# The product of exchanged keys in a windowed attention: made by GpSimd, ahead of the sums that it makes already

## The chip, the cores and the metric

The kernel runs on one core of a Trainium2 chip. A core has five engines that run independently and wait for each other through semaphores: TensorE (matrix products, from SBUF into PSUM), VectorE (called DVE in the profile), ScalarE (ACT), GpSimd (POOL) and SyncE (SP, which here only issues DMAs). The metric is the device time of one execution in microseconds, and the median of several runs. Before the change it is 934.08 us, the median of 3 runs (932.01 to 934.68).

## The reference, cut to what matters

The program is two layers on 4096 tokens (16 sequences of 256) of width 128, all in float32. A layer adds an attention and a mixture of experts to its input. The change lies in the attention of layer 0, for which this is what is computed:

```python
qk, v = split(layernorm(xn) @ w_qkv.T)           # 8 heads of 64; queries and keys are the same projection
bq, bk = buckets(qk) * 64 ** -0.5, look_around(buckets(qk))   # windows of 128
bq = bq * cos(qf) * qs + rotate_half(bq) * sin(qf) * qs
bk = bk * cos(freqs) / scale + rotate_half(bk) * sin(freqs) / scale
sim = where(mask, NEG, bq @ bk.T)
out = softmax(sim) @ bv
out = out.reshape(b, n, 512) @ w_out.T
```

`rotate_half` exchanges the two halves of a head's 64 channels and changes one sign. So a rotated query or key is the sum of two products: the projection times a table of cosines, and the exchanged projection times a table of sines (the sign and the scale are in the tables). The expert part of layer 0 needs a router on the same normalised tokens; layer 1 has a gated attention and 32 experts of its own.

## The kernel before

**Layout.** In attention the channels lie on the 128 partitions (two heads of 64) and the tokens along the free axis. The tokens are worked in 8 groups of 512 (two sequences). For each group there are 4 pairs of heads, so there are 32 *rotations*, n = 0 to 31, each with a tile of 128 x 512 for queries and one for keys. A rotation serves two *steps*, one for each sequence of the group: scores, softmax and product with the values for two heads of one sequence. The loop `for s in range(-3, NS + 1)` (line 547) runs over the 64 steps with three steps of lead.

**A rotation** is in `rotated(n)`, in four parts that are called in different steps:

- TensorE makes the projection `pq` in PSUM (line 381) in an odd step, s = 2n - 7.
- `copied` (lines 391 to 394), in the next step: ACT copies `pq` to the tile `here` in SBUF, and SyncE issues four DMAs that write its blocks of 32 partitions, exchanged, to the tile `there`.
- `near` (line 398), in the same step: DVE makes `q` and `k`, the products of `pq` with the cosine tables. One operand is in PSUM.
- `far` (line 402), in step 2n - 5: DVE makes `sq` and `sk`, the products of `there` with the sine tables. Both operands are in SBUF. The table covers one sequence and is repeated for the second by a broadcast.
- `sums` (line 406), in the same step: `q` plus `sq`, then `k` plus `sk`. For 0 < n < `FREE` = 23 GpSimd makes them, otherwise DVE.

The tiles for `sq`, `sk`, `here` and `there` have two buffers each, those for `q` and `k` three. Scores that use rotation n are first made in step 2n - 3.

**A step** s, in the order in which the kernel is written: TensorE transposes the attention weights of step s (line 460) and ACT copies them out of PSUM (line 467); ACT takes the exponentials of step s + 2 (line 437); DVE does `near` of a rotation where one is due; DVE divides the weights of step s + 1 by their sums, a reciprocal (line 443) and three multiplications of 128 x 256 in SBUF (line 446; ACT does the fourth, line 451); pieces of the layer norm and of the router for a later group; `far`; the scores of step s + 3 on TensorE (line 421), and on DVE four instructions that mask them and take the row maxima out of PSUM (line 427); `sums`; then the product with the values for step s - 1 (line 477), and the projections of later rotations and groups.

**The pieces.** For each group the layer norm and the router are cut into pieces that are put into fixed steps (dictionary `pieces`, line 517), five steps apart from one group to the next. Two of them use GpSimd: `moments` (line 152) and `again` (line 169) raise a 128 x 4 tile to the power -0.5 there, after a short computation on DVE.

**Order.** All this stands under a manual schedule for TensorE, DVE, ACT and GpSimd: each engine executes its instructions in the order in which the program issues them, and waits are added where the data ask for them. From step 41 on GpSimd also issues indirect DMAs that scatter tokens to the experts (line 317); each of these waits for an instruction of ACT in the same step. `FREE` = 23 ends GpSimd's sums before that: rotation 22 is summed in step 39. SyncE issues, beside the exchanges, loads and the zeroing of the scatter's target (line 610).

Of the kernel before, what the change touches and what calls it, by code (L numbers as in the profile page):

```python
# [15 lines left out]
ALU = mybir.AluOpType  # L16
# [31 lines left out]
def two_layers(ctx: ExitStack, tc: tile.TileContext, a: dict, out: bass.AP):  # L48
    nc = tc.nc
# [16 lines left out]
    def mm_tile(name):  # L66
        tags, n = turn
        turn[1] += 1
        return bank(tags[n % len(tags)], name)
# [4 lines left out]
    def load(name, shape, src=None, eng=None, pool=const):  # L74
        t = pool.tile(shape, F32, tag=name, name=name)
        (eng or nc.scalar).dma_start(out=t, in_=a[name] if src is None else src)
        return t
# [17 lines left out]
    sink = load("sink", [P, N], pool=w_a, eng=sp)  # L95
# [236 lines left out]
    with first as pa:  # L332
# [35 lines left out]
        def over(t):  # L368
            return t.unsqueeze(1).to_broadcast([P, 2, N])
# [4 lines left out]
        FREE = 23  # L374

        def rotated(n):

            g, hp = divmod(n, 4)
            h = slice(hp * P, (hp + 1) * P)
            pq = mm_tile(f"pq_{g}_{hp}")  # L380
            nc.tensor.matmul(pq, wqk[:, h], xhTs0[g], start=True, stop=True)
            heads[n] = got = [
                wk.tile([P, 2, N], F32, tag=f"rot{what}", name=f"{what}_{g}_{hp}", bufs=3) for what in "qk"
            ]
            parts = [wk.tile([P, 2, N], F32, tag=f"rots{what}", name=f"s{what}_{g}_{hp}") for what in "qk"]
            here = wk.tile([P, 2, N], F32, tag="here", name=f"here_{g}_{hp}")
            there = wk.tile([P, 2, N], F32, tag="there", name=f"there_{g}_{hp}")

            def copied():

                nc.scalar.copy(here.rearrange("p b n -> p (b n)"), pq)
                for q in range(0, P, 32):
                    to = q ^ 32
                    nc.sync.dma_start(out=there[to : to + 32], in_=here[q : q + 32])

            def near():
                for t, m in zip(got, (cosq, cosk)):
                    nc.vector.tensor_tensor(t, pq.rearrange("p (b n) -> p b n", n=N), over(m), ALU.mult)

            def far():  # L400
                for t, m in zip(parts, (sinq, sink)):
                    nc.vector.tensor_tensor(t, there, over(m), ALU.mult)

            def sums():
                for r, part in zip(got, parts):
                    (nc.gpsimd if 0 < n < FREE else nc.vector).tensor_tensor(r, r, part, ALU.add)  # L406

            later.append(copied)
            turning.append([near, far, sums])


# [89 lines left out]
        with tc.manual_schedule(engines={order.PE, order.DVE, order.Activation, order.Pool}):  # L501
# [45 lines left out]
            for s in range(-3, NS + 1):  # L547
# [60 lines left out]
                if s >= 2 and s % 2 == 0 and s - 2 < NT0:  # L608
                    n = min(2, NT0 - (s - 2))
# [511 lines left out]
```

## Time and profile before

| what | us |
|---|---|
| median of 3 runs | 934.08 (932.01 to 934.68) |
| the profiled execution's own time | 934.61 |
| its span, first to last instruction | 932.8 |
| TensorE busy | 890.2 (95%) |
| DVE busy | 695.9 (75%) |
| ACT busy | 495.4 (53%) |
| GpSimd busy | 280.5 (30%) |
| rotations 1 to 22, `sq` of the first to `sk` of the last | 24.4 to 234.1 |
| scatters of layer 0, first to last start | 242.8 to 339.5 |

The profile is of one execution. Busy time is when an engine's datapath works; register, branch and semaphore instructions and the issue of DMAs do not count. L402 is line 402 of the kernel before. A row for a group of instructions gives the line, the engine, the operation, what it writes and reads (out<-in, buffer numbers left out), the shapes, the count, the busy time and the mean duration of one in nanoseconds, the idle time of the engine just before them and what ended that. A row of the timeline gives start, duration, engine, line, operation and the count of instructions merged into it. Starts are in us from the first instruction. A matmul's end is modelled, and a busy TensorE is not one at its peak; spans on GpSimd are rough.

### The profile page before, as it was taken

To read this page: it belongs to the slowest core of one execution; us is meant where nothing else is said; L and a number is where in the kernel's file an instruction comes from. 1 tells how busy PE (TensorE), PEld (TensorE's weight loads), DVE (VectorE), ACT (ScalarE), POOL (GpSimd) and SP (SyncE) were. 2 spreads that over 40 slices of the span, in tenths; PEclk is the share of its full clock that TensorE was granted. 3 is DMA by queue.
4 is the path that set the end of the run, shared out by engine and by line. 5 is a ranking of instruction groups with operands and counts; after the bars stand their busy time and mean duration, and the time that the engine had idled before them with its cause. 6 is when DMAs were issued, how large, how long until landed. Compare 5 with 4: busy or idle time off the path is not lost.

```text
span 932.8 us, 13465 instructions
## 1 busy us (share of the span) xinstructions
PE 890.2 (95%) x3762; PEld 506.0 (54%) x3762; DVE 695.9 (75%) x2283; ACT 495.4 (53%) x1228; POOL 280.5 (30%) x251
## 2 busy tenths in 40 slices
PE   2999999999999999989999999999999999999997
PEld 1456666565555547888545454454544545445453
DVE  4999999899999933333688686885868858678563
ACT  1688998798898873334443423434234342434411
POOL 2343333322467640001524231242312423121200
PEclk8899999999999999999999999999999999999999
DMA  7171010110122228984172434315343144331430
GB/s 199 27 235 43 24 35 24 25 34 24 44 77 66 69 73 265 260 231 133 29 159 60 112 91 94 91 48 113 90 90 93 49 107 97 81 87 42 104 91 11
DMA packets 70441, 84.54 MB, mean 91 GB/s; under 512 B 14944, under 2 KB 45408, under 8 KB 70240
## 3 DMA queue, kind: packets, MB, share of 16 engines
q1 hardware_dynamic: 65840, 74.76, 31.1%
q0 software_dynamic: 4096, 8.40, 3.0%
q8 instruction: 31, 0.51, 0.2%
q10 hardware_dynamic: 432, 0.53, 0.2%
q14 instruction: 42, 0.34, 0.1%
HBM read 58.22 MB, written 17.04 MB: 81 GB/s over the span
## 4 chain that ended last, share of the span: by engine, by line
PE 61%; DVE 22%; ACT 6%; DMA 4%; issue 3%; SPq 2%; POOL 1%; DVEq 0%; ACTq 0%
PE z L1001 9%; PE g L964 8%; PE u L966 8%; DVE p L427 4%; PE s L421 4%; PE o L477 3%; DVE p L446 3%; PE o L939 3%; PE yr L691 3%; PE h L680 3%; PE t L460 2%; ACT r1s L905 2%; PE y L490 2%; DMA xt<-x_rows 2%; PE z L1019 2%
## 5 line engine op out<-in xcount | busy, mean ns | idle before, releaser
L968 ACT ACTIVATE h<-g 128x512 f32<-128x512 f32 x128 | 75.1, 592 | 204.7 <-PE g L964 201.9
L970 DVE TENSOR_TENSOR h<-h,u 128x512 f32<-128x512 f32 x128 | 86.5, 681 | 61.4 <-PE u L966 45.9
L966 PE MATMUL u<-xn1Ts,eu 128*128 128x512 f32 x256 | 130.8, 593 | 1.2 <-DVE h L970 1.2
L964 PE MATMUL g<-xn1Ts,eg 128*128 128x512 f32 x256 | 130.8, 593 | 0.0
L437 ACT ACTIVATE p<-p,nm 128x256 f32<-128x256 f32 x256 | 127.5, 514 | 0.2 <-DVE nm L427 0.2
L1001 PE MATMUL z<-h,ed 128*128 128x512 f32 x224 | 115.3, 598 | 1.6 <-DVE h L973 0.9
L762 POOL DMA_INDIRECT yg<-y_rows,slot_at x64 | 65.8, 1028 | 117.6 <-PE hs L627 99.0
L973 DVE TENSOR_TENSOR h<-h,bc 128x512 f32<-128x512 f32 x128 | 97.7, 770 | 2.3
L427 DVE CUSTOM_DVE_ANT_0 p<-s,mask 128x256 f32<-128x256 f32 x256 | 92.8, 418 | 2.5 <-PE s L421 2.5
L421 PE MATMUL s<-k,q 64*128 64x256 f32 x512 | 84.3, 411 | 8.7 <-DVE k L406 6.0
L966 PEld LDWEIGHTS u<-xn1Ts,eu 128*128 128x128 f32 x256 | 48.5, 190 | 61.1 <-issue 52.3
L460 PEld LDWEIGHTS t<-ident,p 128*128 128x128 f32 x512 | 59.4, 141 | 35.0 <-issue 8.3
L317 POOL DMA_INDIRECT x_rows<-xn_all,slot_at x64 | 67.1, 1049 | 36.9 <-ACT pT L467 16.0
L467 ACT COPY pT<-t 128x512 f32<-128x512 f32 x128 | 69.2, 597 | 10.4 <-PE t L460 10.4
L1001 PEld LDWEIGHTS z<-h,ed 128*128 128x128 f32 x224 | 41.5, 190 | 55.9 <-issue 39.1
L964 PEld LDWEIGHTS g<-xn1Ts,eg 128*128 128x128 f32 x256 | 46.9, 191 | 45.2 <-issue 39.4
L910 POOL TENSOR_TENSOR r1s<-r1s,sinr 128x512 f32<-128x512 f32 x16 | 21.0, 1312 | 166.4 <-ACT r1s L905 166.3
L477 PE MATMUL o<-pT,v 128*64 128x256 f32 x512 | 70.3, 396 | 0.3 <-ACT oT L482 0.2
L460 PE MATMUL t<-ident,p 128*128 128x128 f32 x512 | 67.3, 274 | 1.4 <-ACT p L451 1.4
L421 PEld LDWEIGHTS s<-k,q 64*128 64x128 f32 x512 | 51.0, 188 | 26.6 <-DVE nm L427 9.0
L446 DVE TENSOR_SCALAR p<-p,sm 128x256 f32<-128x256 f32 x208 | 62.1, 357 | 2.3
L683 ACT ACTIVATE h0s<-h,we 128x256 f32<-128x256 f32 x78 | 32.7, 470 | 53.6 <-issue 43.8
(264 smaller groups left out, 1510.2 us busy)
## 6 DMA issues: line engine op xcount, KB each, us to landing
bc<-rows_r SPq DMA_DIRECT2D x128, 256.0 KB, 4.4
there<-here SPq DMA_DIRECT2D x128, 64.0 KB, 2.0
we<-in_ex_dram SPq DMA_DIRECT2D x39, 129.0 KB, 3.9
xt<-x_rows SPq DMA_DIRECT2D x39, 128.0 KB, 3.9
y_rows<-yt SPq DMA_DIRECT2D x39, 128.0 KB, 3.7
x_rows<-zero SPq DMA_DIRECT2D x19, 256.0 KB, 3.3
x<-in_x_dram SPq DMA_DIRECT2D x8, 256.0 KB, 5.8
out_dram<-out SPq DMA_DIRECT2D x8, 256.0 KB, 2.3
```

Source lines behind the costliest of these rows:

```text
L421: nc.tensor.matmul(sp[h][:, i, :], q[rows, b, i * P : (i + 1) * P], k[rows, b, :], start=True, stop=True)
L427: nc.vector.tensor_tensor_reduce(out=pr[:, h, i, :], in0=sp[h][:, i, :], in1=mask[:, i, :], scale=-1.0, scalar=-NEG, op0=ALU.add, op1=ALU. ...
L437: paces[1] = nc.scalar.activation(row, row, AF.Exp, bias=nm[:, n : n + 1], scale=-1.0, accum_out=sm[:, n : n + 1])
L446: nc.vector.tensor_scalar(row, row, sm[:, n : n + 1], None, ALU.mult)
L460: nc.tensor.transpose(tp[:, at : at + P], pr[:, h, i, j * P : (j + 1) * P], ident)
L477: nc.tensor.matmul(op[h * DH : (h + 1) * DH, :], vs[g][:, 2 * b + j, (2 * hp + h) * DH : (2 * hp + h + 1) * DH], pT[:, h, j, :], start=(j ...
L964: nc.tensor.matmul(gp, wg, xn1Ts[g], start=True, stop=True)
L966: nc.tensor.matmul(up, wu, xn1Ts[g], start=True, stop=True)
L968: nc.scalar.activation(h, gp, AF.Silu)
L970: nc.vector.tensor_tensor(h, h, up, ALU.mult)
L973: nc.vector.tensor_tensor(h, h, spread_w[g][n // 2][:, n % 2, :], ALU.mult)
L1001: nc.tensor.matmul(zp, w, r, start=(n == 1), stop=False)
```

## The change

In `far` the second product, that of the exchanged keys with their sine table, is issued on GpSimd for rotations 1 to 22, and on DVE as before for rotations 0 and 23 to 31. The product of the exchanged queries stays on DVE. The call stays where it was, so on GpSimd the product stands after whatever the pieces of that step have issued there, and ahead of the two sums of the same rotation.

```diff
             def far():
                 for t, m in zip(parts, (sinq, sink)):
-                    nc.vector.tensor_tensor(t, there, over(m), ALU.mult)
+                    eng = nc.gpsimd if m is sink and 0 < n < FREE else nc.vector
+                    eng.tensor_tensor(t, there, over(m), ALU.mult)
```

Everything else is unchanged: tables, buffers, the places of the calls, and the DMAs.

## The prediction

> **What bounds the kernel now.** The change touches rotations 1 to 22 of the attention stage, so I first read busy times by stretch, cut where VectorE (DVE) begins to have idle time. Columns: stretch and length, then each engine's busy time and count, TensorE clock, DMA share, GB/s.
> ```profile
> 28.00:68.00 40.00, 37.07 (x212) 21.95 (x210) 38.95 (x165) 34.71 (x107) 14.71 (x13) 0.99 0.46 145
> 68.00:98.00 30.00, 30.00 (x187) 18.84 (x188) 28.85 (x120) 27.02 (x85) 11.42 (x10) 1.00 0.16 43
> 98.00:127.00 29.00, 29.00 (x178) 18.04 (x177) 28.25 (x117) 26.17 (x82) 10.68 (x9) 1.00 0.11 27
> 127.00:168.00 41.00, 39.21 (x246) 24.24 (x242) 40.09 (x169) 37.41 (x117) 16.10 (x13) 1.00 0.12 30
> 168.00:200.00 32.00, 32.00 (x192) 19.05 (x192) 27.38 (x108) 27.27 (x86) 8.49 (x6) 0.95 0.11 28
> 200.00:236.00 36.00, 35.32 (x203) 21.16 (x202) 34.14 (x138) 31.29 (x96) 10.86 (x8) 1.00 0.10 25
> ```
> From 28 to 168 us DVE is busy 136.1 of 140 us. In the timeline its only gaps over 0.08 us are 1.06 at 28 and 0.18, 0.34 and 0.12 later; the rest are 0.02 to 0.05 between dependent instructions. So DVE sets the pace there, although TensorE looks full too and the chain of waits runs through TensorE from 67 to 127. From 168 to 236 DVE is idle 6.5 us and TensorE leads. DVE time added before 168 therefore lengthens the run nearly one for one; time removed helps only until TensorE leads.
>
> Next the groups that move (count, busy us, mean ns, idle before), on GpSimd (POOL) and on DVE:
> ```profile
> L406 POOL TENSOR_TENSOR q<-q,sq 128x512 f32<-128x512 f32 x22 | 33.1, 1506 | 85.3 <-DVE sq L402 70.7 <-PE t L460 8.5 <-PE s L421 6.0
> L406 POOL TENSOR_TENSOR k<-k,sk 128x512 f32<-128x512 f32 x22 | 28.0, 1271 | 0.0
> ```
> ```profile
> L402 DVE TENSOR_TENSOR sk<-there,sink 128x512 f32<-128x512 f32 x32 | 21.9, 683 | 0.0
> ```
> GpSimd has room: the stretches above hold 72 us of its work in 208. But why is the first sum 0.24 us dearer than the second? It starts while DVE still runs sk. That sent me to places where both engines use SBUF together (start, duration), in layer 1:
> ```profile
> 494.20 1.25 POOL L783 TENSOR_TENSOR x<-x,xn 128x512 f32<-128x512 f32 x1
> ```
> ```profile
> 494.26 1.87 DVE L173 TENSOR_SCALAR xh<-xn,brs 128x128 f32<-128x128 f32 x4 [1.12 <-POOL brs L169]
> ```
> ```profile
> 530.46 1.27 POOL L910 TENSOR_TENSOR r1s<-r1s,sinr 128x512 f32<-128x512 f32 x1
> 531.80 1.59 POOL L912 TENSOR_TENSOR r<-r,r1s 128x512 f32<-128x512 f32 x1
> ```
> ```profile
> 531.10 2.84 DVE L973 TENSOR_TENSOR h<-h,bc 128x512 f32<-128x512 f32 x2
> ```
> Four L173 take 0.86 alone (149.12) and 1.87 here: blocked until 0.18 before the GpSimd sum ends. Two L973 take 1.29 when free (the same shape in L970) and 2.84 here: the first waits 0.48 for L910; then L912, which has been waiting, gets in between the two, and the second waits 1.07. So SBUF-to-SBUF work of either kind on DVE stops while a large GpSimd sum runs. Reductions from PSUM do not: L427 keeps 0.42 under every sum. The 123 divisions L446 before 235 us take 345 to 356 ns each, because no sum of theirs collides: the two sums now fit between sk and the next division, where DVE works from PSUM (L427, L398).
>
> **The change part by part.**
> *Removed from DVE*: one sk per rotation. Starts lie 0.60 apart, so 0.60 each.
> *Added to GpSimd*: one product, 1.27 us by the row r1s<-r1s,sinr (1272 median, same shape, same broadcast factor). Its queue is pow, product, q sum, k sum. The product waits for the exchanged keys, whose DMAs land some 4.4 us after the ACT copy, mostly before DVE reaches sq. So it runs before sq, and what it collides with depends on where the pow of the layer norm (L152, L169) stands.
>
> *Group A, rotations 2, 3, 7, 8, 12, 13: the pow comes one step earlier.* Rotation 2:
> ```profile
> 32.07 1.02 POOL L152 TENSOR_TENSOR brs_a<-bve_a,mhalf 128x4 f32<-128x4 f32 x1 [4.05 <-DVE bve_a L150]
> ```
> ```profile
> 33.52 0.88 DVE L446 TENSOR_SCALAR p<-p,sm 128x256 f32<-128x256 f32 x3
> 34.31 1.11 DVE L158 TENSOR_SCALAR xn_all<-x,bmv_a,brs_a 128x128 f32<-128x128 f32 x4
> 35.34 0.69 DVE L402 TENSOR_TENSOR sq<-there,sinq 128x512 f32<-128x512 f32 x1
> ```
> The keys have landed at 31.9, so the product runs from 33.07 to 34.34. L446 wants to start at 33.52 and starts at 34.16: 0.64 lost, 0.60 saved. For rotation 3 the loss is 0.68. Net +0.06 each, +0.4 for six.
>
> *Group B, rotations 4, 5, 9, 10, 14, 15: the pow is in the same step.* Rotation 4:
> ```profile
> 54.70 0.69 DVE L402 TENSOR_TENSOR sq<-there,sinq 128x512 f32<-128x512 f32 x1
> ...
> 58.69 0.88 DVE L446 TENSOR_SCALAR p<-p,sm 128x256 f32<-128x256 f32 x3
> ```
> ```profile
> 54.75 1.52 POOL L152 TENSOR_TENSOR brs_a<-bve_a,mhalf 128x4 f32<-128x4 f32 x1 [5.47 <-DVE bve_a L150]
> 56.25 1.27 POOL L406 TENSOR_TENSOR q<-q,sq 128x512 f32<-128x512 f32 x1
> 57.48 1.27 POOL L406 TENSOR_TENSOR k<-k,sk 128x512 f32<-128x512 f32 x1
> ```
> The product takes the place of the q sum at 56.25 and pushes the sums to 57.48 and 58.71. L446 comes at 58.09 without sk: it waits for the q sum until 58.57 (0.48), and the k sum gets in among the three divisions, 1.07 as at 531.80. Loss between 0.48 (the divisions stay together) and 1.55; I take 1.55, since the row shows the GpSimd operation entering. Net +0.95. Rotation 15 loses its share after 168, where DVE has idle time, and only its 0.60 counts: 5 x 0.95 - 0.6 = +4.15.
>
> *Group C, rotations 6 and 11: no pow near.* The product starts at the landing (70.7, 120.2) and holds the small two-operand L226 up (71.25 to 71.84); loss 0 to 1, net taken as 0. *Rotations 16 to 22* lose 0 to 0.9 for 0.60 where TensorE leads: 0, bounds -1.5 and +1. *Rotation 1* frees DVE before a wait for ACT (1.06 at 28.11): 0.
>
> *Waits.* The k sum of group B ends at 59.98 instead of 58.74, or up to 1 later; its first score matmul starts at 62.42, and the least room anywhere is 2.8 (rotation 3). If that cover went, TensorE would wait by what is missing. The next pow on GpSimd follows 5 us later, the first scatter at 242.8, after the last changed sum (236.45). SyncE's exchange DMA two rotations on must now also wait for GpSimd's read, long over: 0. Nothing else moves in a queue.
>
> *Sum*: 0.4 + 4.15 = +4.5 on the profiled execution, which took 934.61 (span 932.8) and stands 0.5 above the median of 934.08. I take half a microsecond off: TensorE's idle 1.79 at 165.64 is followed by 3.4 us at half clock, about 1.7 lost, and rotation 15's 0.60 may shorten that idle enough to avoid it (idle 1.39 at 252.54 had no such sequel), though new gaps can bring others. 934.1 + 4.0 = 938.1.
>
> [...]
>
> **Rivals.**
> 1. *Faster: the divisions are not held.* L446 is never seen under a GpSimd sum; L173 is its nearest row, and against this. Then DVE saves 14 x 0.60 = 8.4 before 168, less what TensorE cannot follow: its idle and late score groups there come to some 12, not all of DVE's making. Gain about 7: 927. It decides this way when the mean loss per rotation is under 0.3.
> 2. *A wash: the k sum does not break into the divisions.* Group B loses 0.48 and nets -0.12: with group A about -0.8, within 2 of before: 933. For it: three divisions follow closer (0.26) than two L973 (0.6). Against: at 531.80 the waiting engine got in.
> 3. *Worse: blocks multiply.* Group C and rotations 16 to 22 lose a full 1.1 each, net +0.5 x 9, or two more half-clock spells of 1.7: 942 to 943.
> 4. *GpSimd's sums become late and scores wait.* It needs over 2.8 of delay on one rotation; I find 1.2 to 2.2. If it came, some 2 us each in group B: 948; 3 in 100.
>
> **How the numbers follow.** About 0.3%, 2.8 us, can be told from no change. Chances: forecast 0.54 (936 to 941), rival 1 0.15, rival 2 0.18, rivals 3 and 4 0.13. Slower by over 2.8: four fifths of the forecast, all of 3 and 4, a little of 2: 0.58. Faster: rival 1 and some of 2: 0.18. Same: 0.24. The range reaches from the upper part of rival 1, 930, to the end of rival 3, 943.5.
>
> **What would show it.** Of the profile after: 22 GpSimd products near 1.27; L402 sk only 10 times on DVE. L446 groups of three at 1.5 instead of 0.88 in group A, above 1.3 in group B; all 0.88 would make rival 1 right. A split group of three in B shows the k sum inside. TensorE's busy share from 28 to 168 falls. Wrong it would be if DVE's idle time before 168 grows, or if landings come late, so that sq and the product meet.

## The result and the profile after

The kernel got slower: a median of 942.22 us (939.25 to 946.28, 7 runs) against 934.65 (932.01 to 936.17, 7 runs) for before in the same runs. The ratio is 1.0086 with a 95% interval of 1.0067 to 1.0104, that is 6 to 10 us. The profiled execution took 943.73, its span is 941.9.

Busy time by stretch of the kernel after, cut at the same times as before (columns: stretch and length, then TensorE, its weight loads, DVE, ACT and GpSimd with counts, TensorE clock, DMA share, GB/s):
```profile
28.00:68.00 40.00, 36.22 (x209) 21.58 (x208) 39.03 (x159) 33.82 (x104) 16.96 (x15) 0.99 0.44 139
68.00:98.00 30.00, 28.70 (x166) 17.18 (x168) 27.22 (x104) 24.09 (x75) 14.18 (x12) 0.94 0.18 50
98.00:127.00 29.00, 28.37 (x168) 17.29 (x164) 28.41 (x103) 25.84 (x79) 14.39 (x11) 1.00 0.11 28
127.00:168.00 41.00, 40.23 (x244) 24.92 (x244) 39.97 (x165) 35.52 (x110) 17.34 (x14) 1.00 0.11 27
```
DVE is nearly as full as before (134.6 us of 140 against 136.1), though 14 products of 0.60 us are gone from it, and TensorE gets through fewer matmuls (787 in place of 823). The 1.5 us by which DVE is idle longer lie between 68 and 98, where TensorE fell to half clock (a granted clock of 0.50 for 3.41 us from 76.30). What fills DVE instead is one group, here from the page's costliest groups (count, busy us, mean ns, idle before):
```profile
L447 DVE TENSOR_SCALAR p<-p,sm 128x256 f32<-128x256 f32 x208 | 77.9, 431 | 2.3
```
These are the divisions of line 446 of before, where 208 of them took 62.1 us, 357 ns each: 15.8 us more, with nothing changed in them. GpSimd's groups cost what was expected, near 1.27 each (same columns):
```profile
L403 POOL TENSOR_TENSOR sk<-there,sink 128x512 f32<-128x512 f32 x22 | 28.4, 1290 | 22.2 <-DMA there<-here 22.1
L407 POOL TENSOR_TENSOR k<-k,sk 128x512 f32<-128x512 f32 x22 | 28.3, 1286 | 0.0
L407 POOL TENSOR_TENSOR q<-q,sq 128x512 f32<-128x512 f32 x22 | 28.0, 1275 | 47.4 <-DVE sq L403 32.5 <-PE t L461 12.0 <-PE o L478 2.9
```
The q sum is even 0.23 us cheaper than before, since DVE's sk no longer runs beside its start: of the 22 q sums before, the 16 that started under sk took 1.56 to 1.65 and the 6 that did not 1.26 or 1.27. The two engines get into each other's way.

*Group A*, rotation 2, the timelines of GpSimd and of DVE after (start, duration):
```profile
31.94 1.02 POOL L152 TENSOR_TENSOR brs_a<-bve_a,mhalf 128x4 f32<-128x4 f32 x1 [4.42 <-DVE bve_a L150]
32.93 1.27 POOL L403 TENSOR_TENSOR sk<-there,sink 128x512 f32<-128x512 f32 x1
```
```profile
33.47 1.42 DVE L447 TENSOR_SCALAR p<-p,sm 128x256 f32<-128x256 f32 x3
34.81 1.10 DVE L158 TENSOR_SCALAR xn_all<-x,bmv_a,brs_a 128x128 f32<-128x128 f32 x4
35.83 0.68 DVE L403 TENSOR_TENSOR sq<-there,sinq 128x512 f32<-128x512 f32 x1
```
Three divisions that took 0.88 take 1.42: the first starts at 33.47 under the product, which ends at 34.20, and takes 0.89 alone; the other two take 0.34 each, as they do when free. The other five rotations of the group show 1.52 or 1.53.

*Group B*, rotation 4, the same two timelines:
```profile
54.68 1.52 POOL L152 TENSOR_TENSOR brs_a<-bve_a,mhalf 128x4 f32<-128x4 f32 x1 [5.18 <-DVE bve_a L150]
56.18 1.27 POOL L403 TENSOR_TENSOR sk<-there,sink 128x512 f32<-128x512 f32 x1
57.41 1.27 POOL L407 TENSOR_TENSOR q<-q,sq 128x512 f32<-128x512 f32 x1
58.64 1.32 POOL L407 TENSOR_TENSOR k<-k,sk 128x512 f32<-128x512 f32 x1
```
```profile
57.82 0.17 DVE L444 RECIPROCAL sm<-sm 128x4 f32<-128x4 f32 x1
58.02 2.35 DVE L447 TENSOR_SCALAR p<-p,sm 128x256 f32<-128x256 f32 x3
```
The product takes 56.18, where the q sum began before; the sums move back by one place, and the divisions, which come at 58.02, meet the q sum and then the k sum: 2.35 or 2.36 in place of 0.88, in all six rotations of the group. The reciprocal at 57.82 also works from SBUF to SBUF, and it is not held: it runs under the q sum in 0.17, as it does when no GpSimd operation runs. So not all such work stops.

*Group C*, rotation 6, DVE and GpSimd:
```profile
69.44 2.35 DVE L447 TENSOR_SCALAR p<-p,sm 128x256 f32<-128x256 f32 x3
71.71 1.50 DVE L212 TENSOR_TENSOR gt_r<-gt_r,eq_r 128x256 f32<-128x256 f32 x1
```
```profile
71.66 1.28 POOL L403 TENSOR_TENSOR sk<-there,sink 128x512 f32<-128x512 f32 x1 [0.29 <-DMA there<-here]
```
The divisions of rotation 5's group B have made DVE late, so the next product now meets a router instruction with two SBUF operands, which takes 1.08 us more than its 0.42 before. Rotation 11 does the same to L204 (1.49 in place of 0.42).

### The profile page after: what moved, and what is told of

It is laid out like the page before. It is cut to its first block, busy times and chain, and to the rows that moved or that the text cites. A ratio compares the mean times of both kernels' runs of the same rounds, so it can differ in the third digit from the quotient of the medians.

```text
span 941.9 us, 13500 instructions
## 1 busy us (share of the span) xinstructions
PE 895.5 (95%) x3762; PEld 507.8 (54%) x3762; DVE 702.6 (75%) x2261; ACT 496.3 (53%) x1228; POOL 303.3 (32%) x273
## 4 chain that ended last, share of the span: by engine, by line
PE 59%; DVE 21%; ACT 7%; DMA 6%; issue 4%; SPq 2%; POOL 1%; DVEq 0%; ACTq 0%; POOLq 0%
PE z L1002 9%; PE u L967 8%; PE g L965 8%; PE s L422 4%; PE o L478 4%; DVE p L428 4%; DVE p L447 3%; DMA xt<-x_rows 3%; PE o L940 3%; PE t L461 2%; ACT r1s L906 2%; PE yr L692 2%; PE h L681 2%; PE pq L381 2%; PE y L491 2%
## 5 line engine op out<-in xcount | busy, mean ns | idle before, releaser
L447 DVE TENSOR_SCALAR p<-p,sm 128x256 f32<-128x256 f32 x208 | 77.9, 431 | 2.3
```

Source lines behind the costliest of these rows:

```text
L447: nc.vector.tensor_scalar(row, row, sm[:, n : n + 1], None, ALU.mult)
```

## The experiments

My theory (the expectations call it the port theory; the name is a label only, and no run shows by what means the one engine stops the other): DVE's elementwise work between SBUF and SBUF, the divisions above all, stops while a large GpSimd operation runs, so a product that leaves DVE costs what it blocks, and that depends on where it falls. Rivals: GpSimd's sums become late because one more operation stands in its queue (queue); the difference is TensorE's half-clock spells, the stretches in which the profile shows a granted clock of 0.5 (clock). Three runs split the change by rotations. In each, one line differs:

```diff
-                    eng = nc.gpsimd if m is sink and 0 < n < FREE else nc.vector
+                    eng = nc.gpsimd if m is sink and n in (2, 3, 7, 8, 12, 13) else nc.vector       # group A alone
+                    eng = nc.gpsimd if m is sink and n in (4, 5, 9, 10, 14, 15) else nc.vector      # group B alone
+                    eng = nc.gpsimd if m is sink and n in (1, 6, 11, *range(16, FREE)) else nc.vector   # the rest
```

The experiments ran on other chips, on which the median of before is 944 to 950 us; each ratio is against before on the same chip. Their traces fall behind that of before after rotation 26, where the scatters run. So I also read from each trace when the first score matmul of a rotation starts, less the same in the trace of before, in us:

```
rotation                 1     4     5     6     9    10    11    14    15    16    22
the change            -0.05  0.80  1.79  3.98  4.03  5.87  6.46  6.50  6.78  6.78  5.62
the change, again      0.03  1.26  2.24  2.83  2.89  4.72  5.31  5.35  4.04  4.04  2.88
group A alone          0.16  0.05  0.05  0.05  0.09  0.09  0.09  0.15 -1.45 -1.45 -1.44
group B alone          0.55  1.42  1.30  1.89  1.91  2.67  3.62  3.62  3.90  3.90  3.91
the rest alone        -0.15 -0.04 -0.03  0.33  0.33  0.33  0.78  0.77 -0.81 -0.81 -1.97
B, pow behind sums     0.17  0.55 -0.05 -0.05  0.82  0.38  0.38  1.41 -0.73 -0.73 -0.71
no product at all     -0.23 -1.11 -1.71 -1.64 -2.42 -2.86 -2.86 -3.47 -5.61 -5.61 -6.77
earlier products      -0.52 -1.02 -1.62 -1.56 -1.20 -1.64 -1.64 -2.24 -4.36 -4.37 -5.51
earlier, pow behind   -0.20 -0.96 -1.57 -1.57 -1.19 -1.63 -1.63 -2.24 -4.38 -4.38 -5.54
extra product          0.27  2.49  3.67  4.26  5.49  7.47  8.42  9.49 10.58 10.58 12.07
fill                  -0.28  1.45  1.45  1.81  2.11  3.48  4.43  4.80  3.96  4.08  4.09
```

The step of some -1.4 at rotation 15 is before's own half-clock spell at 168.5, which several traces do not have.

**Group A alone.**

> Only the six rotations of group A (2, 3, 7, 8, 12, 13) have their key product on GpSimd. Port theory (SBUF-to-SBUF work of VectorE stops while a GpSimd product or sum reads SBUF): each of the six groups of three divisions takes 1.4 to 1.55 us in place of 0.88, 0.65 lost for 0.60 saved, so the time stays within 1.5 us of before. Queue theory (the cost comes from GpSimd's sums being made later, behind one more operation): six of 22 rotations, so about 6/22 of the 7.6 us, +2 us. Clock theory (the cost is half-clock spells of TensorE that come by chance): within 2 us, with spells in number like before.

944.48 us against 943.87; ratio 1.0021 (0.9998 to 1.0045). The interval leaves room for 0 and for the queue theory's 2 us; the trace does not: divisions at 1.26 to 1.53 in the six places, 0.88 in all others up to 240 us (later ones, under the scatters, take up to 1.12 before too), and no delay from rotation 1 to 14 (0.16 and 0.15). Loss and saving cancel.

**Group B alone.**

> Only the six rotations of group B (4, 5, 9, 10, 14, 15) have their key product on GpSimd. Port theory: six groups of divisions at 2.35 us in place of 0.88, 1.47 lost for 0.60 saved, five of them before TensorE leads: 5 x 1.47 - 6 x 0.60 = +3.8 us, 3 to 5.5 with one more half-clock spell. Queue theory: 6/22 of 7.6, +2 us, and no more than group A. Clock theory: within 2 us.

948.06 us; ratio 1.0044 (1.0021 to 1.0067), +4.2. Six groups of divisions at 2.35 or 2.36, all others 0.88 up to 240. The table has +3.1 from rotation 1 to 14. The same number of products as in group A on the same engine costs four microseconds or next to nothing, by its place. The clock theory falls here: its bound was 2 us, and TensorE has one half-clock spell between 30 and 300 us, as before has.

**The rest alone.**

> Only the other ten rotations (1, 6, 11, 16 to 22) have their key product on GpSimd. Port theory: rotations 6 and 11 lose up to 1.1 each on a small two-operand instruction for 0.60 saved, the others lie where VectorE has idle time: -1 to +1.5 us. Queue theory: 10/22 of 7.6, +3.5 us. Clock theory: within 2 us.

945.34 us; ratio 1.0012 (0.9982 to 1.0042). Rotations 6 and 11 cost 0.36 and 0.45 in the trace: without group B's delay the product holds L226 there, as the prediction had it, to 0.95 and 1.02 in place of 0.19. Rotations 19 and 21 gain 0.6 each, where TensorE leads. The time alone would not exclude 3.5; the trace is at -2.0 at rotation 22, -0.6 without the spell.

**The product left out.** The sums use the query product for both:
```diff
                 for t, m in zip(parts, (sinq, sink)):
-                    nc.vector.tensor_tensor(t, there, over(m), ALU.mult)
+                    if m is sinq or not 0 < n < FREE:
+                        nc.vector.tensor_tensor(t, there, over(m), ALU.mult)
...
-                for r, part in zip(got, parts):
+                for r, part in zip(got, parts if not 0 < n < FREE else parts[:1] * 2):
```

> The key product of rotations 1 to 22 is left out altogether; GpSimd adds the query product to the keys in its place (so the keys are wrong), and GpSimd does only its two sums, as before. It shows what relief of VectorE alone is worth. If VectorE is the bound from 28 to 168 us, 14 x 0.60 = 8.4 us come off it there, and TensorE's own waits limit what is left of that: -4 to -7 us. If TensorE is the bound there, as its full busy share and the chain of waits suggest: 0 to -2 us.

937.25 us against 943.87; ratio 0.9916 (0.9889 to 0.9943), -8 us (6.6 by the medians). Some 3 us of this are clock by my estimate: these six runs have a mean clock of 0.994 against 0.991 for before, and 0.0033 of 940 us is 3.1. The trace has -3.2 from rotation 1 to 14 and -6.5 to rotation 22, about 1.4 of it the spell at 168.5. So the relief is worth some 4 to 5 us, and DVE does bound much of the stage. The 3.2 by rotation 14 are less than 13 products of 0.60, or 7.8, and the trace shows two reasons. DVE waits 3.5 us for ACT from 28 to 168, against 1.6 before. And it comes earlier to the divisions of group B, where the k sum, though not moved, now catches them. Rotation 4:
```profile
57.12 1.34 DVE L447 TENSOR_SCALAR p<-p,sm 128x256 f32<-128x256 f32 x3
```
The k sum ends at 57.78 there, and 0.46 is lost; the six places show 1.15 to 1.34. So of the 1.47 that a rotation of group B loses in the change, 0.46 would be lost by DVE's being early alone, and 1.0 comes of the pushed sums.

**One more product, nothing taken away.**
```diff
                     nc.vector.tensor_tensor(t, there, over(m), ALU.mult)
+                if 0 < n < FREE:
+                    spare = wk.tile([P, 2, N], F32, tag="spare", name=f"spare_{g}_{hp}")
+                    nc.gpsimd.tensor_tensor(spare, there, over(sink), ALU.mult)
```

> VectorE does all its products as before, and GpSimd makes the key product of rotations 1 to 22 a second time, into a scratch tile that nobody reads, at the place where the change has it. So VectorE is relieved of nothing. Port theory: the losses of the change without its savings: +4.4 (rotations 2 to 15 in the change) + 8.4 (14 x 0.60) = +13, less what the shifted positions spare, 10 to 16 us. If the cost of the change came from keys that are ready later, it would be the change's own +7.

956.44 us against 944.30; ratio 1.0122 (1.0081 to 1.0164), +11.5. Divisions are at 1.17 to 2.97 at the places of the change and 0.88 elsewhere up to 240. A product that nobody reads makes the kernel slower by more than the change does: the cost lies in what the operation stops on DVE. The sums are pushed here too, so this run alone does not exclude late keys. The trace of the change does: from 29 to 245 us no instruction waits for a sum of GpSimd.

**A fill in place of the product.** DVE works as before; GpSimd writes zeros when the keys have landed (the waits for the four DMAs are left out here):
```diff
+                if 0 < n < FREE:
+                    spare = wk.tile([P, 1024], F32, tag="spare", name=f"spare_{g}_{hp}", bufs=1)
+                    ins = nc.gpsimd.memset(spare, 0.0)
```

> As before, but at the place of the moved product GpSimd fills a scratch tile of 128 x 1024 with zeros (some 1.2 us by the fill of 128 x 256 in 0.31), when the exchanged keys have landed: an operation of the same length that reads nothing from SBUF. If it is reading that blocks, groups of three divisions keep 0.88 under a fill; if any GpSimd operation on SBUF blocks, they take 1.4 or more. In group B the sums are pushed into the divisions either way (1.3 or more).

It took 958.58 us, in a single run, which I use for its trace alone. GpSimd and DVE in rotation 2:
```profile
33.18 0.95 POOL L407 MEMSET spare<- 128x1024 f32 x1
```
```profile
33.62 1.18 DVE L457 TENSOR_SCALAR p<-p,sm 128x256 f32<-128x256 f32 x3
```
The fill reads nothing and still costs the divisions 0.30, which is what is left of it when they come (34.13 - 33.62 = 0.51), less 0.2: under the products of the change too, the first division loses 0.19 or 0.20 less than what is left (0.54 of 0.73 at 33.47, 0.65 of 0.85 at 43.05). The six places of group A show 1.17 or 1.18; the expectation of 1.4 took the fill to last 1.2, and it lasts 0.95. So reading is not needed to block this kind of instruction.

**Group B with the pow behind the sums.** As group B alone, and in odd steps the pow is issued last on GpSimd:
```diff
-        nc.gpsimd.tensor_tensor(rs, ve, mhalf, ALU.pow)
+        root(lambda: nc.gpsimd.tensor_tensor(rs, ve, mhalf, ALU.pow))     # and so the other pow
...
+                behind_sums[0] = s > 0 and s % 2 == 1                      # root() then only notes it
...
                 if sums:
                     sums()
+                behind_sums[0] = False
+                drain(roots)
```

> Group B alone, as in the run with group B alone, but in odd steps the pow of the layer norm is issued behind GpSimd's two sums instead of ahead of the product. The product then starts at the landing of the keys and the sums follow sq at once. If group B's cost is that the pow and the product push the sums into the next group of divisions (port theory), these groups are back at 0.88 us in steps 4, 6, 14, 16, 24 and 26, rotations 5, 10 and 15 lose up to 1 us each on the layer norm's SBUF-to-SBUF instructions, and the time is within 2 us of before, against +4 with group B alone. If one more operation of GpSimd costs whatever its place, it stays at +4.

952.46 us against 950.46; ratio 1.0018 (0.9993 to 1.0043). GpSimd and DVE around rotation 4 and the product of rotation 5:
```profile
55.72 1.28 POOL L415 TENSOR_TENSOR q<-q,sq 128x512 f32<-128x512 f32 x1 [3.35 <-DVE sq L411]
56.95 1.28 POOL L415 TENSOR_TENSOR k<-k,sk 128x512 f32<-128x512 f32 x1
58.19 1.02 POOL L160 TENSOR_TENSOR brs_a<-bve_a,mhalf 128x4 f32<-128x4 f32 x1
60.53 1.27 POOL L411 TENSOR_TENSOR sk<-there,sink 128x512 f32<-128x512 f32 x1 [1.32 <-DMA there<-here]
```
```profile
58.27 0.88 DVE L455 TENSOR_SCALAR p<-p,sm 128x256 f32<-128x256 f32 x3
...
60.06 2.08 DVE L166 TENSOR_SCALAR xn_all<-x,bmv_a,brs_a 128x128 f32<-128x128 f32 x4
```
The sums end at 58.23, the divisions start at 58.27, and all of them are back at 0.88. The loss has moved: the next product breaks into the four normalisations (2.08 for 1.1), and two later ones, at 100.2 and 149.5, hold a scaling of the layer norm (L181) to 1.3 for 0.28. The trace has +1.2 from rotation 1 to 14 in place of group B's +3.1.

**Products one step earlier.** For rotations 2 to 22 the product is issued in the even step, ahead of a pow there, or else with a wait for the last normalisation or router instruction of DVE, so that it runs while DVE reads PSUM:
```diff
+            def early():
+                ins = nc.gpsimd.tensor_tensor(parts[1], there, over(sink), ALU.mult)
+                if marks[0] is not None:
+                    tc.add_manual_dep(ins.ins, marks[0].ins.name, ...)
...
+                product = earlies.pop((s + 6) // 2, None) if s % 2 == 0 else None
+                if product and s in (-2, 0, 8, 10, 18, 20):
+                    product()
+                    product = None
                 for n in pieces.get(s, ()):
                     step(routing, n)
+                if product:
+                    product()
```

> The key products of rotations 2 to 22 are on GpSimd, but issued one step earlier: in the even step ahead of the pow of the layer norm where there is one, otherwise behind the last two-operand or SBUF-to-SBUF piece of VectorE (a wait is added), so that they run while VectorE takes the row maxima out of PSUM. Rotation 1 stays on VectorE. Port theory: groups of three divisions in even and odd steps near 0.88 us again, except in group B, where the k sum still meets the division of the next step (0.5 each); VectorE is relieved of some 0.5 per rotation, and the time falls 2 to 6 us below before. Queue theory (more work in GpSimd's queue costs by itself): as slow as the change, +5 to +8.

941.18 us against 944.30; ratio 0.9980 (0.9952 to 1.0009). Group A's divisions are at 0.88 to 0.92, group B's at 1.13 to 1.35. The 1.9 us gained are just under the 2 to 6 expected, and the interval includes 0; the queue theory's +5 to +8 is excluded.

**The same, with the pow behind the sums in odd steps.**

> As the kernel with the earlier products, and in odd steps the pow of the layer norm is issued behind the two sums, so that group B's sums are not pushed against the divisions. Port theory: no group of divisions over 1.0 us in rotations 2 to 15; 0 to 2.5 us faster than with the earlier products alone, 4 to 7 below before. Queue theory: as slow as the change.

940.75 us; ratio 0.9970 (0.9943 to 0.9997), -2.8 us: faster than before, just clear of no change, and the fastest kernel here that computes everything, but short of the 4 to 7 expected. GpSimd and DVE in rotation 2:
```profile
32.44 1.28 POOL L414 TENSOR_TENSOR sk<-there,sink 128x512 f32<-128x512 f32 x1 [4.03 <-DMA there<-here]
33.68 1.10 POOL L160 TENSOR_TENSOR brs_a<-bve_a,mhalf 128x4 f32<-128x4 f32 x1
```
```profile
33.87 0.88 DVE L466 TENSOR_SCALAR p<-p,sm 128x256 f32<-128x256 f32 x3
```
The product ends at 33.72, the divisions start at 33.87; the pow that runs beside them does not hold them (0.88, as in a free group). In rotations 2 to 15 the longest groups are 1.20 and 1.01. Against the products alone the second step shows nothing in the time: group B's divisions are freed, yet the table's rows are the same to 0.1 from rotation 4 to 22.

**The change again, beside others.**

> The change itself, on the chip and beside the runs of before that the other experiments share: +7 to +8 us if the parts add up (group A alone +2.0, group B alone +4.2, the rest alone +1.1, each within 2.5) and if nothing of the difference was the first chip's. Half-clock spells of TensorE: more of them than in before would leave some 5.5 us at equal clock.

955.88 us against 950.46; ratio 1.0068 (1.0041 to 1.0094), +6.5 by the ratio and 5.4 by the medians. The parts add up to +7.3 (2.0 + 4.2 + 1.1, each within 2.5). This trace has no spell in the attention's first 300 us, and is 5.3 us late at rotation 14. The mean clock of these runs is that of before beside them (0.988 each).

## Why the prediction was right, and where its sizes were off

The direction, the mechanism and the range held: 938.1 forecast, 942.2 measured, 930 to 943.5 given. The size did less well: +7.6 by the medians where +4.0 was forecast, close to the upper end. By its steps:

- *DVE bounds the stage from 28 to 168.* Right in the main: leaving the product out gives some 4 to 5 us beside the clock, of 8.4 taken off. DVE's idle time before 168, whose growth was to be a sign of being wrong, rises from 3.9 to 5.4 in the profiled execution and to 4.3 in the second trace, which has no spell there.
- *Group A, loss 0.64 to 0.68 for 0.60.* Measured 0.54 and 0.65 on the divisions; alone, the six together delay the scores by nothing where 0.4 was forecast.
- *Group B, loss 1.55 with the k sum inside the divisions, against 0.48.* Measured 1.47: the k sum does get in. Steps of 0.87, 0.98 and, for rotations 9 and 10 together, 1.83 in the start of the scores (the change again), as forecast (0.95 each); rotation 14 shows no step there. With the pow put behind the sums the divisions are back at 0.88.
- *Group C, loss 0 to 1, net 0.* This term was too small. 1.08 and 1.07 were lost, on L212 and L204 and not on L226: group B's delay of DVE moved it against the landing. Without group B (the rest alone) L226 is held. Net +0.6 for each (2.24 to 2.83 and 4.72 to 5.31 in the change again), +1.2 together.
- *Sum.* Up to rotation 14 the terms forecast are 0.4 + 5 x 0.95 = 5.1, and 4.5 with rotation 15's 0.60. Measured 5.3 at rotation 14 without spells. That this comes so close is in part luck: group C's 1.2 makes up for group A and rotation 14.
- *Rotations 16 to 22, 0.* They gained 1.2 (6.78 to 5.62), though divisions took 1.17 to 1.89 there: TensorE leads and DVE's stops are hidden, as assumed.
- *Half a microsecond off for the clock.* In the profiled execution this step failed in sign. The spell after the idle time at 165 was not avoided, and more came, at 76 and 260. In the second trace of the change none came before 300, so the half microsecond was a bet on chance. The stretches of TensorE around the last one, after:
```profile
257.20:260.60 3.40, 2.00 (x15) 1.00 0.09 27
260.60:267.50 6.90, 6.90 (x25) 0.51 0.09 30
```
In the table the one at 76 is seen at rotation 6, 2.19 in the change against 0.59 again, and the one at 260 takes 3.25 in the profiled execution, between rotations 23 and 24. Nothing in the change shows as the cause of the one at 260: the code there is the same, and TensorE waits 1.40 us for the same instruction as before (1.39), after which before went on at full clock. The runs of the change go from 939.25 at a mean clock of 0.991 to 946.28 at 0.983; the three at 0.991 and 0.992 average 940.1, which is 5.4 over the median of before, whose profiled execution has 0.991. On the other chip, at equal mean clocks, the change costs 5.4 by the medians and 6.5 by the ratio. So I estimate some 5.4 us for held DVE work, net of the relief, and some 2 for the clock. Whether and which gaps set off a spell is open: in the trace of before, a stretch of 3.40 us with TensorE busy for 2.14 (from 250.40) had no spell behind it, and in that of the change, one of 3.50 with 2.21 busy (from 72.80) had one.

Of the rivals, the faster one (divisions not held) and the wash (the k sum stays out) are excluded by the 1.42 and 2.35. Rival 3, that blocks multiply, came in part: group C and the spells. Rival 4, late keys, did not come: in the trace after, nothing waits for GpSimd's sums from 29 to 245 us.

The L173 row, on which the loss of group A was worked out, was a good guide: it has DVE blocked until 0.18 before the GpSimd sum ends. Under the product at 32.93, the divisions at 33.47 had 0.73 to go until its end at 34.20, and they lost 0.54, 0.19 less. That divisions belong to the work that is held, for which before had only the nearest row, L173, is now shown by 0.88 against 1.42 to 2.35.

## What to carry to other kernels

Before giving GpSimd an elementwise operation in order to relieve DVE, list what DVE does while it will run: here work that reads PSUM went on (in the trace of the change, row maxima at 0.41 to 0.43 and `near` at 0.68 to 0.69 under its products and sums), and multiplications and two-operand work from SBUF to SBUF stopped (three divisions at 1.42 to 2.35 for 0.88, L212 at 1.50 for 0.42), while a small reciprocal did not (128 x 4, 0.17). 0.60 saved cost 0.54 to 1.47, and nearly the same products (rotation 1 stayed on DVE) with a place under PSUM work turned +0.7 to 0.9% into -0.3%. And an operation inserted ahead of others in GpSimd's queue moves those too: more than half of the loss (6 x 1.47 of 14.7 us in the three groups) came where sums that had just fitted were pushed 1.2 us on and DVE came 0.6 earlier. Taking work off one engine moves it against the others too: the 0.46 was lost even with no product on GpSimd.

## What the runs showed of the hardware that I had not expected

- A GpSimd fill that reads nothing holds DVE's SBUF-to-SBUF multiplications as a product does (1.18 in place of 0.88 for three, under a fill of 0.95).
- The length of GpSimd's operation alone does not decide: with the earlier products and the pow behind the sums, a pow of 128 x 4 takes 1.10 us, and three divisions that start 0.19 into it take 0.88, as when free; under a fill of 0.95 they take 1.18.
- A GpSimd operation that waits gets in between two DVE instructions that otherwise start 0.26 to 0.27 us apart: in the groups of three at 2.35 the first division takes 0.81 under the q sum, the second 1.36 under the k sum, which got in between them, and the third 0.34.
- In the trace of the change TensorE fell to half clock (0.50 or 0.51) for 3.41 us from 76.30, after a stretch of 3.50 with 1.29 idle, for 3.45 from 175.30, after 3.50 with 1.77 idle, and for 6.9 from 260.60, after 3.40 with 1.40 idle. In the trace of before a stretch of 3.40 with 1.26 idle went on at full clock: a wait of 1.40 for the same instruction was followed by half clock in one trace, and one of 1.39 was not in the other.
- Chips differ by 9 to 16 us for the same kernel (before, by medians: 934.65 on the first, 943.87, 944.30 and 950.46 on the others). Of the two traces of the change, the one of the slower chip falls 13.3 us behind from rotation 26 on; the indirect DMAs run there, but that they are the cause is not shown.
